# Matmul order in the four-tile passes of two expert mixtures around a slot-attention layer

## The chip, the core and the metric

The kernel runs on one core of a Trainium2 chip. A core has five engines with a program of their own each: TensorE (PE in the profile; PEld is its weight load), VectorE (DVE), ScalarE (ACT), GpSimd (POOL) and SyncE (SP, which here issues DMAs). Each takes its instructions in a fixed order and waits on semaphores for the others. The metric is the device time of one execution in microseconds, the median of the runs.

## The reference

Two sequences of 1024 tokens of 512 features go through three layers with residuals: half a mixture of two experts, an attention of 16 heads with 64 memory slots, and half a mixture again with the same weights. The mixture is what the change touches:

```python
h = jnp.einsum('nd,ehd->enh', x_flat, w_fc)                 # 512 -> 2048 hidden, two experts
a = jnp.square(jnp.where(h >= 0, h, 0.5 * h))
expert_out = jnp.einsum('enh,edh->end', a, w_proj)          # 2048 -> 512
mask = (top_idx[None, :] == jnp.arange(num_experts)[:, None]).astype(x.dtype)
out = jnp.einsum('end,en->nd', expert_out, mask * top_weight[None, :])
```

All is float32. A token uses one expert; the first `einsum` is called the first layer here and the second the second layer.

## The kernel before

**Passes.** Tokens are sorted by expert into a DRAM buffer. A mixture works through 17 tiles of 128 sorted tokens in six passes, each of which belongs to one expert. Lines 44 and 45 give the tiles of each pass: (2, 4, 2, 4, 1, 4) in the first mixture, (4, 4, 4, 2, 2, 1) in the last. Pass numbers count from 0. A pass runs over four chunks of 512 hidden features (`NHQ`, loop variable `ck`). For each chunk the weights `wfc` and `wp` are loaded by SP into a pool of 11 large buffers.

**Slow and fast passes.** Passes of one or two tiles use plain matmuls: `hidden` (bank hp, L514) and `project` (banks op, L735). Passes of four tiles use a scheme with seven block products in place of eight: `hidden_fast` (L598) for the first layer and `project_fast` (L664) for the second. Its operands are sums of blocks: T of tokens (DVE), S and R of the weights (POOL, L545 to L573), Q of the activations (DVE, `unit_sums`, L576). T, S, R share a pool of six buffers named sums, so POOL can make the sums of a later chunk only when an older sum has been used for the last time.

**One chunk of the first layer.** `hidden_fast` makes the four activations a of a chunk in two halves, q = 0 and 1. A half has seven products of two matmuls each, in banks named hU, hV and hC, and hands control back (`yield`) four times:

| step of a half | products on TensorE | what reads the banks |
|---|---|---|
| 1 | hU, hV, hC | ACT copies hU (kp or kv), DVE adds hC into hA (L627) |
| 2 | hU again, added to what is there | ACT copies hU (e) |
| 3 | hU again | ACT copies hU (uT), DVE adds it to hV into hB (L636) |
| 4 | hU again (hU<-T,wfc in the trace) | ACT copies hU into hB (L639), DVE t_b (L503), ACT a_b |
| 5 | hV again (hV<-xsT,S) | DVE adds hV and e into hA (L643), DVE t_a (L503), ACT a_a |

Steps 5 of q = 0 and 1 of q = 1 stand together, so a chunk has eight gaps where control comes back. The sums Q of a half are queued in `late` and issued behind the L627 add of the next half. hU and hV share two buffers of one pool, so the next half's hU and hV wait for the readers of the old ones. hU<-T, hV, hU, hV, hC, the last two products of a chunk and the first three of the next, are called a hand-over below.

**Between the steps.** The generator `pending` holds the second layer of the chunk before. `project_fast` has seven products of four matmuls, into banks that a reader empties (oa, in the two pools at and tr) and banks that gather over the pass (o), and yields after each matmul, 28 times. The loop at L794 takes three of these after each first-layer step of a fast pass; the rest follow after the last step (L814):

```python
for _ in steps:
    run(pending, 3 if fast else 0)
    run(ending, 1 if fast else 2)
    run(prep, 0 if early else 1 if fast else 2)
    yield ps, ck
```

`ending` is `finish_fast`, the last sums of the pass before (DVE), and `prep` transposes the tokens of the next pass in its last chunk (bank lt, in pool tr).

**What sets the order.** The program gives instructions with their data dependences. At build time a scheduler simulates the engines and gives each engine its final order: among the instructions that are ready in its simulation it takes the one that the source has first. So a later matmul can move ahead of an earlier one that waits. `tc.issue_after(x)` adds an edge without a wait: what is issued inside it stands behind x on x's engine. The attention layer chains all its TensorE instructions so (`on_pe`, L954); the mixtures do not. The last mixture's pass 0 runs interleaved with the end of the attention layer.

Of the kernel before, what the change touches and what calls it, by code (L numbers as in the profile page):

```python
# [15 lines left out]
P = 128  # L16
# [29 lines left out]
NPASS = 6  # L46
# [3 lines left out]
def tile_macaron(  # L50
# [14 lines left out]
    nc = tc.nc  # L65
# [15 lines left out]
    def large_tile(shape, name):  # L81
        return large.tile(shape, F32, tag="big", name=name)
# [139 lines left out]
    def small_t(shape, tag, name, dt=F32, bufs=2):  # L222
        return small.tile(shape, dt, tag=tag, name=name, bufs=bufs)
# [8 lines left out]
    class Mixture:  # L232
# [3 lines left out]
        def __init__(self, ph, plan, split):  # L236
            self.ph, self.rows, self.split = ph, None, split
            self.passes, self.groups = plan
            self.starts = [sum(self.passes[:j]) for j in range(NPASS)]
            self.e1 = small_t([P, NT], "e1", f"e1{ph}")  # L240
            self.run = small_t([P, NT], "run", f"run{ph}")
            self.before = small_t([P, NT], "bef", f"bef{ph}")
            self.pos = small_t([P, NT], "pos", f"pos{ph}", mybir.dt.int32)

            self.own = small_t([P, NPASS], "own", f"own{ph}")
            self.seen = self.ranked = self.done = 0
            self.deferred = not split

# [206 lines left out]
    def ffn(m, views):  # L457
# [36 lines left out]
        def activate(h, hc, nm, psum=False):  # L494
            n = h.shape[-1]
            t = work.tile([P, n], F32, tag="sq", name=f"t{nm}")
            if psum:

                r = work.tile([P, n], F32, tag="th", name=f"r{nm}")
                nc.scalar.activation(r, h, AF.Relu, scale=0.5)  # L500
                m.mark_dve = nc.vector.scalar_tensor_tensor(t, h, 0.5, r, ALU.mult, ALU.add)  # L501
            else:
                m.mark_dve = nc.vector.scalar_tensor_tensor(t, h, 0.5, h, ALU.mult, ALU.max)  # L503
            at = work.tile([P, n], F32, tag=A_TAGS[hc], name=f"a{nm}", bufs=3)
            nc.scalar.activation(at, t, AF.Square)
            return at
# [16 lines left out]

# [65 lines left out]
        def flush():  # L594
            while late:
                late.pop(0)()

        def hidden_fast(ps, ck, xT, T, wfc, S, a, sums):  # L598
            w = wfc.rearrange("p (k d h) -> p k d h", k=2, d=2)
            lo, hi = slice(0, 256), slice(256, 512)  # L600
            a += [None] * 4
            for q in range(2):
                nm = f"{ph}_{ps}_{ck}_{q}"
                first, second = ts(q, P), slice(256 + q * P, 256 + (q + 1) * P)
                U = ps2.tile([P, 256], F32, tag="pj", name=f"hU{nm}")
                V = ps2.tile([P, 256], F32, tag="pj", name=f"hV{nm}")
                C = ps1.tile([P, 256], F32, tag="st", name=f"hC{nm}")

                def product(bank, left, right, start):
                    for d in range(2):  # L610
                        m.mark = nc.tensor.matmul(  # L611
                            bank, lhsT=left[:, d, :], rhs=right[:, d, :],
                            start=start and d == 0, stop=d == 1, skip_group_check=True,
                        )

                def keep(name, bufs=2):
                    t = work.tile([P, 256], F32, tag=name, name=f"{name}{nm}", bufs=bufs)
                    nc.scalar.copy(t, U)  # L618
                    return t

                hA = work.tile([P, 512], F32, tag="oT", name=f"hA{nm}")
                hB = work.tile([P, 512], F32, tag="oT", name=f"hB{nm}")
                product(U, w[:, 0, :, first], xT[:, 0:2, lo], True)
                p1 = keep(("kp", "kv")[q], 1)
                product(V, S[0][:, :, first], T[0], True)
                product(C, w[:, 1, :, first], xT[:, 2:4, lo], True)
                added = nc.vector.tensor_tensor(hA[:, lo], C, p1, ALU.add)  # L627
                with tc.issue_after(added.ins):
                    flush()
                yield  # L630
                product(U, S[1][:, :, first], T[1], False)
                u2 = keep("e")
                yield
                product(U, S[2][:, :, first], T[2], False)
                u3 = keep("uT")
                nc.vector.tensor_tensor(hB[:, hi], V, u3, ALU.add)  # L636
                yield
                product(U, w[:, 1, :, second], T[3], False)
                nc.scalar.copy(hB[:, lo], U)  # L639
                a[q + 2] = activate(hB, q + 2, nm + "b")  # L640
                yield
                product(V, S[3][:, :, first], xT[:, 2:4, hi], False)
                nc.vector.tensor_tensor(hA[:, hi], V, u2, ALU.add)  # L643
                a[q] = activate(hA, q, nm + "a")
                late.append(lambda q=q: sums.append(unit_sums(ps, ck, q, a)))
# [18 lines left out]
        def project_fast(ps, ck, a, S, wp, R, p, raw):  # L664
            w = wp.rearrange("p (k q d) -> p k q d", k=2, q=2)
            lo, hi = slice(0, 256), slice(256, 512)
            nm = f"{ph}_{ps}_{ck}"
            if ck == 0:
                for i, (pool, tag) in enumerate(OP_TAGS[1:]):
                    p[i] = pool.tile([P, 2, 256], F32, tag=tag, name=f"o{i}_{nm}")  # L670
                p["sum"] = large_tile([P, 4, 2, 256], f"osum_{nm}")
            acc = p["sum"]


            def product(bank, left, right, first, last):
                for t in range(2):
                    for q in range(2):
                        nc.tensor.matmul(  # L678
                            bank[:, t, :], lhsT=left(q)[:, ts(t, P)], rhs=right(q),
                            start=first and q == 0 and (t == 0 or last),  # L680
                            stop=last and q == 1, skip_group_check=True,
                        )
                        yield

            def keep(i, left, right):
                yield from product(p[i], left, right, ck == 0, ck == NHQ - 1)

            def add(i, left, right):

                pool, tag = ((ps2, "at"), (ps1, "tr"))[i % 2]  # L690
                bank = pool.tile([P, 2, 256], F32, tag=tag, name=f"oa{i}_{nm}")
                yield from product(bank, left, right, True, True)
                if ck == 0:
                    nc.scalar.copy(acc[:, i], bank)
                else:
                    nc.vector.tensor_tensor(acc[:, i], bank, acc[:, i], ALU.add)

            yield from add(0, lambda q: a[q][:, lo], lambda q: w[:, 0, q, lo])
            yield from keep(0, lambda q: a[q + 2][:, lo], lambda q: w[:, 1, q, lo])
            yield from add(1, lambda q: S[q][1], lambda q: R[1][:, q, :])  # L700
            yield from keep(1, lambda q: S[q][3], lambda q: w[:, 1, q, hi])
            yield from add(2, lambda q: S[q][2], lambda q: R[2][:, q, :])
            yield from keep(2, lambda q: a[q + 2][:, hi], lambda q: R[3][:, q, :])
            yield from add(3, lambda q: S[q][0], lambda q: R[0][:, q, :])
# [42 lines left out]
        def run(steps, n):  # L747
            for _ in range(n if steps else 0):
                next(steps, None)

        pending = ending = None
        late = []
        for ps in range(NPASS):
            fast = PASSES[ps] == 4
            ops = {} if fast else []
            for ck in range(NHQ):
                if ps == 0 and ck == 0:
# [34 lines left out]


                for _ in steps:  # L794
                    run(pending, 3 if fast else 0)
                    run(ending, 1 if fast else 2)
                    run(prep, 0 if early else 1 if fast else 2)
                    yield ps, ck
# [23 lines left out]
                if fast:  # L822
                    pending = project_fast(ps, ck, a, products, wp, R, ops, raw)
                else:
                    pending = project(ps, ck, a, wp, ops, raw)
# [601 lines left out]
    for _ in norm:  # L1427
        pass
    last_steps = ffn(last_mixture, out_views)
    attention(att, last_mixture, last_steps, weight_steps)  # L1430
    for _ in last_steps:
# [46 lines left out]
```

## Time and profile before

| | |
|---|---|
| median of 3 runs | 2293.77 us (2293.19 to 2294.2) |
| profiled execution | 2291.76 us |
| span of that execution, first to last instruction | 2290.1 us |
| mean granted TensorE clock | 0.996 |
| HBM traffic over the span | 97 GB/s |
| first mixture, fast pass 1 | 84 to 181.5 us |
| first mixture, fast pass 3 | 250.3 to 343.6 us |
| first mixture, fast pass 5 | 382.2 to 488 us |
| attention layer | from about 488 us to about 1870 us |
| last mixture, fast passes 1 and 2 | 1934 to 2031 and 2031 to 2129 us |

Times in the trace count from the first instruction of the span. An answer of the timeline names, for each group, its start, its duration, the engine, the line, the operation, the tile written and the tiles read, the shapes and how many records it has; in brackets stands how long the engine had been idle and what ended it. A float32 matmul leaves two records. Records of TensorE overlap, since matmuls are pipelined: the distance from one start to the next is the time that a matmul costs, 0.43 us for two records of 256 columns. The number behind a tile's name is left out, so hU stands for the hU of every chunk.

### The profile page before, as it was taken

How to read it: one execution, taken by the hardware profiler on the slowest of the kernel's cores; microseconds unless marked ns; L12 is line 12 of the kernel's file. 1: busy time of each engine (PE TensorE's matmuls, PEld its weight loads, DVE VectorE, ACT ScalarE, POOL GpSimd, SP SyncE). 2: the span in 40 equal slices, each digit the busy share in tenths (PEclk: the TensorE clock that was granted, in tenths of full speed). 3: DMA queues.
4: the chain of work that ended last, by engine and by line, in shares of the span. 5: the costliest groups of instructions: out<-in, count | busy, mean ns of one | idle time of the engine just before them, and what ended most of it. 6: DMA issues, size and time to landing. Idle time of an engine off the chain costs nothing.

```text
span 2290.1 us, 28873 instructions
## 1 busy us (share of the span) xinstructions
PE 2224.7 (97%) x10776; PEld 1533.8 (67%) x10776; DVE 1360.2 (59%) x3124; ACT 778.4 (34%) x1526; POOL 473.2 (21%) x400
## 2 busy tenths in 40 slices
PE   6999999999999999999999999999999999999998
PEld 5687687866556656655665656656655678888765
DVE  6554555656556656666865655755657777675311
ACT  2222222323434343444443433443433332222222
POOL 3523615301101101100101000000001345444000
PEclk9999999999999999999999999999999999999999
DMA  7615525331221311310312110210110303322442
GB/s 285 232 59 205 195 77 223 115 124 37 90 90 56 134 47 65 106 70 24 129 56 74 56 41 29 74 33 19 56 38 1 111 33 148 126 86 102 170 175 102
DMA packets 56940, 222.75 MB, mean 97 GB/s; under 512 B 5983, under 2 KB 13151, under 8 KB 38880
## 3 DMA queue, kind: packets, MB, share of 16 engines
q1 hardware_dynamic: 51232, 203.52, 25.1%
q0 software_dynamic: 5280, 16.85, 1.9%
q8 instruction: 86, 1.41, 0.2%
q10 hardware_dynamic: 288, 0.52, 0.1%
q14 instruction: 54, 0.44, 0.1%
HBM read 189.86 MB, written 31.54 MB: 97 GB/s over the span
## 4 chain that ended last, share of the span: by engine, by line
PE 75%; DVE 13%; issue 6%; ACT 2%; POOL 2%; DMA 1%; SPq 1%; another core or an unknown queue 0%; POOLq 0%; DVEq 0%; ACTq 0%
PE U L956 9%; PE po L956 7%; PE oa L678 7%; PE hU L611 6%; PE kU L956 6%; PE o L678 5%; PE V L956 5%; PE pq L956 4%; PE hp L514 4%; PE hV L611 3%; PE op L735 3%; PE C L956 2%; PE svp L956 2%; PE AB L956 2%; PE ok L956 2%
## 5 line engine op out<-in xcount | busy, mean ns | idle before, releaser
L1253 POOL TENSOR_TENSOR sg<-sg,ms 128x512 f32<-128x512 f32 x64 | 68.5, 1071 | 1147.3 <-DVE ms L1251 1062.2
L956 PE MATMUL po<-wo,oT 128*128 128x512 f32 x512 | 230.3, 592 | 0.0
L514 PE MATMUL hp<-xsT,wfc 128*128 128x256 f32 (+1 forms) x768 | 150.7, 351 | 8.1 <-DVE t L501 3.6
L956 PEld LDWEIGHTS po<-wo,oT 128*128 128x128 f32 x512 | 94.8, 190 | 93.7 <-issue 91.8
L514 PEld LDWEIGHTS hp<-xsT,wfc 128*128 128x128 f32 x768 | 128.3, 193 | 32.0 <-issue 10.6
L735 PE MATMUL op<-wp,a 128*128 128x512 f32 x320 | 143.2, 593 | 0.0
L1249 ACT ACT_TABLE_LOAD x63 | 80.8, 1283 | 146.8 <-DVE ms L1248 140.8
L501 DVE SCALAR_TENSOR_TENSOR t<-hp,r 128x256 f32<-128x256 f32 (+1 forms) x96 | 36.3, 378 | 154.1 <-ACT r L500 151.9
L956 PE MATMUL U<-vgT,X 128*128 128x512 f32 x256 | 120.3, 592 | 0.0
L1149 DVE RECIPROCAL rC<-CT 128x256 f32<-128x256 f32 x64 | 112.2, 1753 | 2.2
L956 PE MATMUL pq<-xnT,wq 128*128 128x512 f32 x256 | 113.0, 592 | 0.0
L956 PE MATMUL kU<-ksT,X 128*128 128x256 f32 x384 | 102.1, 388 | 1.4 <-DVE E L1049 1.4
L735 PEld LDWEIGHTS op<-wp,a 128*128 128x128 f32 x320 | 59.7, 190 | 60.9 <-issue 57.2
L611 PE MATMUL hU<-xsT,wfc 128*128 128x256 f32 x384 | 99.2, 380 | 0.7 <-ACT e L618 0.7
L1179 DVE TENSOR_REDUCE mx<-ts 128x4 f32<-128x256 f32 x64 | 27.0, 422 | 106.1 <-PE ts L956 105.9
L956 PEld LDWEIGHTS pq<-xnT,wq 128*128 128x128 f32 x256 | 48.3, 190 | 59.3 <-issue 58.6
L956 PEld LDWEIGHTS kU<-ksT,X 128*128 128x128 f32 x384 | 67.9, 190 | 27.1 <-issue 12.5
L500 ACT ACTIVATE r<-hp 128x256 f32<-128x256 f32 (+1 forms) x96 | 33.2, 347 | 154.9 <-PE hp L514 151.0
L1182 ACT ACT_TABLE_LOAD x63 | 80.8, 1283 | 1.1
L611 PEld LDWEIGHTS hU<-xsT,wfc 128*128 128x128 f32 x384 | 71.7, 190 | 13.7 <-issue 3.5
L956 PEld LDWEIGHTS U<-vgT,X 128*128 128x128 f32 x256 | 48.6, 190 | 47.5 <-issue 45.9
L1100 ACT COPY kET<-tk 128x512 f32<-128x512 f32 x64 | 37.4, 585 | 125.7 <-PE tk L956 125.7
(301 smaller groups left out, 5075.7 us busy)
## 6 DMA issues: line engine op xcount, KB each, us to landing
wfc<-in_w_fc_dram SPq DMA_DIRECT2D x48, 1024.0 KB, 5.0
wp<-in_w_proj_dram SPq DMA_DIRECT2D x48, 1024.0 KB, 6.7
vgT<-vgs SPq DMA_DIRECT2D x16, 1024.0 KB, 5.2
wv<-in_w_v_dram SPq DMA_DIRECT2D x8, 1024.0 KB, 6.0
ksT<-kss SPq DMA_DIRECT2D x8, 1024.0 KB, 5.0
wo<-in_w_o_dram SPq DMA_DIRECT2D x8, 1024.0 KB, 4.8
xs<-xs SPq DMA_DIRECT2D x6, 1032.0 KB, 5.1
wks<-in_w_ks_dram SPq DMA_DIRECT2D x24, 256.0 KB, 3.1
```

The source lines that it names most:

```text
L500: nc.scalar.activation(r, h, AF.Relu, scale=0.5)
L501: m.mark_dve = nc.vector.scalar_tensor_tensor(t, h, 0.5, r, ALU.mult, ALU.add)
L514: m.mark = nc.tensor.matmul(hp, lhsT=wfc[:, dc * HQ + hc * P : dc * HQ + (hc + 1) * P], rhs=xT[:, dc, :], start=(dc == 0), stop=(dc == DC ...
L611: m.mark = nc.tensor.matmul(bank, lhsT=left[:, d, :], rhs=right[:, d, :], start=start and d == 0, stop=d == 1, skip_group_check=True,)
L678: nc.tensor.matmul(bank[:, t, :], lhsT=left(q)[:, ts(t, P)], rhs=right(q), start=first and q == 0 and (t == 0 or last), stop=last and q == ...
L735: nc.tensor.matmul(ops[j], lhsT=a[hc][:, ts(j, P)], rhs=wp[:, ts(hc, D)], start=(ck == 0 and hc == 0), stop=(ck == NHQ - 1 and hc == HQ // ...
L956: att.pe = op(*args, **kw)
L1100: nc.scalar.copy(u.kET, tp)
L1149: nc.vector.reciprocal(u.rC, u.CT)
L1182: nc.scalar.activation(u.u, u.u, AF.Exp)
L1249: nc.scalar.activation(ms, ms, AF.Sqrt, bias=eps, scale=1.0 / DV)
L1253: u.gated = then.gated = nc.gpsimd.tensor_tensor(sg, sg, ms.to_broadcast([P, HG, DV]), ALU.mult)
```

## The change

A helper `in_order` chains matmuls as `on_pe` does, for both layers of fast passes, while `m.alone` is true: in passes 0 to 4 of the first mixture and in passes 1 to 5 of the last. Fast among these are passes 1 and 3 of the first mixture and passes 1 and 2 of the last, four of the six fast passes. Transposes and the matmuls of slow passes are not chained. In all six fast passes the loop takes four matmuls of `pending` after each step instead of three, a whole product.

```diff
@@ class Mixture
             self.deferred = not split
+            self.pe, self.alone = None, False
@@ ffn
+        def in_order(op, *args, **kw):
+            with tc.issue_after(m.pe.ins) if m.pe else nullcontext():
+                r = op(*args, **kw)
+            m.pe = r if m.alone else None
+            return r
@@ hidden_fast
-                        m.mark = nc.tensor.matmul(
-                            bank, lhsT=left[:, d, :], rhs=right[:, d, :],
+                        m.mark = in_order(
+                            nc.tensor.matmul, bank, lhsT=left[:, d, :], rhs=right[:, d, :],
@@ project_fast
-                        nc.tensor.matmul(
-                            bank[:, t, :], lhsT=left(q)[:, ts(t, P)], rhs=right(q),
+                        in_order(
+                            nc.tensor.matmul, bank[:, t, :], lhsT=left(q)[:, ts(t, P)], rhs=right(q),
@@ the loop over passes
             fast = PASSES[ps] == 4
+            m.alone = ps < NPASS - 1 if m.split else ps > 0
@@ the loop over steps
-                    run(pending, 3 if fast else 0)
+                    run(pending, 4 if fast else 0)
```

## The prediction

> **What bounds the kernel now.** I read engine shares first, then the table by stretch, then TensorE's timeline at places where one chunk of the hidden layer hands over to the next.
>
> ```profile
> PE 2224.7 (97%) x10776; PEld 1533.8 (67%) x10776; DVE 1360.2 (59%) x3124; ACT 778.4 (34%) x1526; POOL 473.2 (21%) x400
> ...
> PE 75%; DVE 13%; issue 6%; ACT 2%; POOL 2%; DMA 1%; SPq 1%; another core or an unknown queue 0%; POOLq 0%; DVEq 0%; ACTq 0%
> ```
>
> TensorE is busy for 97% of the span and carries 75% of the chain that ended last. The four stretches the change orders (passes 1 and 3 of the first mixture, 1 and 2 of the last) have even less air:
>
> ```profile
> 84.00:181.50 97.50, 95.22 (x425) 78.71 (x424) 58.13 (x90) 25.57 (x57) 41.68 (x30) 1.00 0.29 104
> 250.30:343.60 93.30, 92.55 (x414) 77.40 (x413) 48.89 (x83) 24.09 (x54) 34.04 (x26) 1.00 0.28 98
> 1934.00:2031.00 97.00, 96.63 (x455) 84.46 (x454) 67.59 (x106) 25.27 (x56) 46.72 (x36) 1.00 0.28 95
> 2031.00:2129.00 98.00, 97.58 (x457) 85.58 (x456) 62.15 (x101) 25.18 (x55) 40.25 (x30) 1.00 0.29 102
> ```
>
> Length and TensorE's busy time come first, then PEld, DVE, ACT, POOL, the granted clock (1.00). Idle: 2.3 + 0.75 + 0.4 + 0.4 = 3.8 us of 386. The change removes no matmul, so it can win about that, and every new wait on this engine lengthens the run.
>
> **What covers a hand-over today.** One hand-over of pass 1 of the last mixture (columns: start, duration, engine, line, op, records, idle before):
>
> ```profile
> 2000.24 1.03 PE L611 MATMUL hU<-T,wfc 128*128 128x256 f32 x4
> ...
> 2001.36 0.37 ACT L639 COPY hB<-hU 128x256 f32<-128x256 f32 x1 [1.79 <-PE hU L611]
> ...
> 2001.76 0.69 DVE L503 SCALAR_TENSOR_TENSOR t_1b<-hB 128x512 f32<-128x512 f32 x1 [1.06 <-ACT hB L639]
> ...
> 2002.40 1.03 PE L611 MATMUL hV<-xsT,S 128*128 128x256 f32 x4
> ...
> 2003.46 0.42 DVE L643 TENSOR_TENSOR hA<-hV,e 128x256 f32<-128x256 f32 x1 [1.01 <-PE hV L611]
> ...
> 2004.99 1.03 PE L611 MATMUL hU<-xsT,wfc 128*128 128x256 f32 x4
> ...
> 2005.23 1.27 POOL L553 TENSOR_TENSOR S<-wfc 128x512 f32<-128x512 f32 x1 [14.79 <-PE oa L678]
> ...
> 2005.85 1.03 PE L611 MATMUL hV<-T,S 128*128 128x256 f32 x4
> ```
>
> A first-layer product is four records, 0.86 us from its start to the next. Three second-layer matmuls (1.30 us) lie between 2001.10 and 2002.40, four (1.73 us) between 2003.26 and 2004.99. The next chunk's hV at 2005.85 can start only when DVE has run t_1b and then the add hA that reads the old hV; hA ended at 2003.88, two microseconds early. Those seven matmuls are the cover.
>
> **The change, part by part.** A second-layer chunk is 7 products of 4 matmuls, 28; a first-layer chunk offers 8 gaps. Three per gap used 24 and left 4 for the end: every gap and the hand-over had filler. Four per gap use all 28 in seven gaps. The eighth, between the last hU<-T and the last hV, is empty, and so is the hand-over: hU<-T, hV, hU, hV, hC run bare. The order edges forbid pulling later matmuls into the hole. Other gaps grow from 1.30 to 1.73 us; they had no wait, so nothing is gained.
>
> *Hand-overs.* The bare sequence stands once in the trace, from 261.50 in the first mixture's pass 3: hV at 262.36, hU at 263.23, hV at 264.09, hC at 265.02. Three products took 2.66 us for 2.59: cost 0.07, with t_0b at 0.69. It stands again in pass 1, beside weight sums on POOL:
>
> ```profile
> 106.36 1.13 PE L611 MATMUL hV<-xsT,S 128*128 128x256 f32 x4 [0.22 <-DVE hB L636]
> ...
> 106.58 2.89 DVE L503 SCALAR_TENSOR_TENSOR t_1b<-hB 128x512 f32<-128x512 f32 x1 [0.27 <-ACT hB L639]
> ...
> 109.95 1.10 PE L611 MATMUL hV<-T,S 128*128 128x256 f32 x4 [1.60 <-DVE hA L643]
> ```
>
> There it cost 109.95 - 107.33 - 0.86 = 1.76. So ends of 0.07 and 1.76, and what decides is whether POOL runs beside t_1b. Between them is the commonest disturbed case:
>
> ```profile
> 2027.45 1.27 POOL L567 TENSOR_TENSOR R<-wp 128x512 f32<-128x512 f32 x1 [16.97 <-PE hU L611]
> ...
> 2027.86 1.40 DVE L503 SCALAR_TENSOR_TENSOR t_1b<-hB 128x512 f32<-128x512 f32 x1 [1.06 <-ACT hB L639]
> ```
>
> 1.40 for 0.69 adds 0.71: a disturbed hand-over costs 0.78. The Trainium skill ("SBUF — State Buffer", section on SBUF's two sides) speaks against this harder: a DVE instruction with two SBUF inputs and a GpSimd one exclude each other for a whole instruction. With POOL starting 1.3 us ahead (below), t_1b waits out the second POOL instruction (1.60, L554) and ends about 1.7 later than alone: 1.7 a hand-over. The row shows half of that; I take the row and keep 1.7 for the range.
>
> Which are disturbed? Two already have t_1b at 1.40 (1928.60, 2027.86). Five more have POOL waiting for a freed sums buffer, which comes just after t_1b today: on hV at 130.78, 293.31, 1979.33 and 2078.64, on oa at 2005.23. The last seven-product matmul (R's last use) now ends before hU<-T instead of after hV, so I expect an R buffer to free first and POOL to start about 1.3 us before t_1b. Seven at 0.78 and five at 0.07 make 5.8. Behind the waiting hV stand hC and the next chunk's products. a_1a, needed 3.0 us after hV ends, takes 0.62 + 0.04 + 0.69 + 0.04 + 0.63 + 0.05 = 2.1: hidden.
>
> *First chunk of passes 1 and 3, first mixture.* The filler there is the two-tile pass before: 8 matmuls of 512 columns. They fill two gaps instead of three, and today's schedule then pulls hC and the next chunk's second-layer matmuls forward; the edges forbid that. A bare step from hU to hU costs: ACT's copy starts 0.20 after the product's end (259.98 after 259.78), lasts 0.37, restart 0.07, 0.64 in all. Three such steps are 1.9. The last hV of the chunk waits for hB behind four sums Q (0.42 + 1.49 + 1.49 + 0.43 in that stretch): about 1.1. With 0.1 more in pass 3 that is 3.1, against 1.4 lost there today (0.57 + 0.07 + 0.73); in pass 1 the same list, 0.2 more at the first hV and its 1.6 hand-over (t_1b 2.89) make 4.9 against 3.2 (0.25 + 0.39 + 1.76 + 0.55 and some 0.3 of slips). Together +3.5; ends 0 (the sums slip) and +6.
>
> *Smaller.* In the last mixture's passes 1 and 2, finish_fast's DVE instructions (0.69 each, at 1953.11 and 1954.32) lie around t_1b at the first hand-over; with no cover one of them shows in part, 0.3 each, 0.6 (ends: -0.8, the 0.42 and 0.37 waits on hA at 2044.19 and 1944.88 vanish; +1.4). In four last chunks a transpose's copy (0.58) must clear bank tr one product before oa needs it: 0.1 each, 0.4. First-mixture pass 5 and last-mixture pass 0 get the new count without edges; the schedule can still fill holes: 0, ends -2 and +2. SP's weight loads: wp is released up to 2 us earlier, nobody waits. The slow passes' hp matmuls keep their order; their second bank is wanted 2.6 us after the last hV starts; hA is done at 1.5 (2003.88 after 2002.40).
>
> *Sum.* 5.8 + 3.5 + 0.6 + 0.4 = +10.3. The profiled execution took 2291.76 (span 2290.1 and 1.7 around it), so 2302.1; the median of the runs stands 2.0 above that execution: **2304**.
>
> **Rivals.** Measurement here can tell about 0.2%, 4.6 us, from nothing.
>
> *No visible change.* POOL's five starts do not move early and the sums slip out of the way: 2 hand-overs at 0.78, ten at 0.07, half of the first-chunk cost: 1.6 + 0.7 + 1.75 = 4.0, so 2298. For it: three of four ordered passes have no wait after their first chunks. Against: the empty gap is certain arithmetic. Chance 0.20.
>
> *Faster.* One mechanism: whole products free the oa banks and let their DVE adds run early, so DVE is clear when hB and hA come. Pass 5's first chunk now waits 2.85 + 0.40 + 0.21 (402.05 on hB, 405.75, 393.75), pass 0's 0.71 + 0.88 (1897.32, 1916.61). All of it gone, plus the 0.79 of hA waits, is -5.8, with hand-overs at 0.07 -5.0: 2289. It decides only if t_1b is never disturbed and the first chunks cost nothing. Against: the 2.85 comes from Q at 3.54 beside POOL, which no order of matmuls touches. Chance 0.10.
>
> *Clearly slower.* The lock as the skill states it: 7 at 1.7 and the rest as above, 11.9 + 0.35 + 4.5, so 2311; if a_1a also comes late, 2316. Chance 0.15.
>
> *The forecast*: 0.55. The order edges take effect in any case, because nothing else can hold the matmuls.
>
> **How the numbers follow.** Slower holds forecast and last rival, 0.70; same 0.20; faster 0.10. The range starts at 2293 (hand-overs at 0.07, first chunks 0, unordered passes -2) and ends at 2316.
>
> **What would show it.** Right: bare hU<-T, hV, hU, hV, hC at each hand-over, hV waiting for DVE hA L643 about ten times, S or R on POOL starting before t_1b, t_1b's median above 0.69; idle of TensorE up by some 1.7 in each of passes 1 and 3, 3 in the last mixture's two. Wrong: t_1b stays at 0.69 and hV waits under 0.1 (no visible change), or the waits of pass 5 are gone (faster).

## The result, and the profile after

| | before | after |
|---|---|---|
| median of the runs | 2293.85 us (8 runs) | 2301.37 us (8 runs) |
| lowest to highest | 2292.97 to 2296.16 | 2299.33 to 2305.42 |
| profiled execution, its span | 2291.76, 2290.1 | 2305.42, 2303.7 |
| mean granted clock | 0.996 | 0.994 |

The ratio is 1.0033, with a 95% interval of 1.0024 to 1.0041: **7.5 us slower**, where 10.3 were forecast. The profiled execution is the slowest of the eight, so sizes taken from it are on the large side. Lines of the kernel after are about ten higher (all chained matmuls of both layers carry L529, the helper's line).

First the shares and the chain of the page, then the table by stretch for the four ordered passes (length, then the busy time of TensorE, its weight load, VectorE, ACT and POOL, the granted clock, the DMA share and GB/s):

```profile
PE 2234.1 (97%) x10776; PEld 1536.2 (67%) x10776; DVE 1363.2 (59%) x3124; ACT 779.6 (34%) x1526; POOL 474.9 (21%) x400
...
PE 75%; DVE 13%; issue 6%; ACT 2%; POOL 2%; DMA 1%; SPq 0%; another core or an unknown queue 0%; POOLq 0%; DVEq 0%; ACTq 0%
```

```profile
86.10:193.30 107.20, 100.87 (x434) 82.01 (x433) 60.10 (x91) 25.86 (x57) 37.86 (x29) 0.97 0.27 91
261.68:358.60 96.92, 95.42 (x430) 79.25 (x429) 49.00 (x86) 24.49 (x55) 34.14 (x26) 1.00 0.28 97
1943.00:2043.40 100.40, 99.87 (x465) 85.94 (x465) 69.33 (x108) 26.60 (x57) 50.74 (x37) 1.00 0.30 100
2043.40:2145.00 101.60, 101.11 (x470) 87.56 (x469) 64.96 (x105) 26.84 (x58) 43.74 (x31) 1.00 0.32 104
```

The page's shares tell nothing of the change. The table does: idle of TensorE is 6.3, 1.5, 0.5 and 0.5 us where it was 2.3, 0.75, 0.4 and 0.4, and only in the first stretch has the clock fallen, to 0.97.

A finer measure is used from here on. From each distance between two starts on TensorE I take off what a record of that width costs undisturbed (216 ns for 256 columns, 430 for 512, 110 for 128); the rest is **loss**, be it a wait or half clock. Summed by place, in the profiled execution of each kernel (the labels are those of the experiments below):

| loss in us | before | after | e_edges | e_four | e_swap_r | e_first | v_best |
|---|---|---|---|---|---|---|---|
| pass 1, chunks 0 and 1 | 3.4 | 10.6 | 4.4 | 9.4 | 7.7 | 2.0 | 0.8 |
| pass 3, chunks 0 and 1 | 1.4 | 2.7 | 2.4 | 1.1 | 3.4 | 0.5 | 0.0 |
| pass 5, chunks 0 and 1 | 4.3 | 8.9 | 5.8 | 9.3 | 3.8 | 2.6 | 2.5 |
| later chunks of passes 1 and 3 | 0.1 | 0.9 | 0.1 | 0.9 | 0.9 | 0.9 | 0.1 |
| join of pass 5 with the attention (35 us) | 8.6 | 1.9 | 8.7 | 1.9 | 1.9 | 1.9 | 1.9 |
| last mixture, pass 0 | 10.9 | 10.3 | 10.9 | 10.4 | 11.0 | 10.4 | 12.6 |
| last mixture, passes 1 and 2 | 1.7 | 3.8 | 2.6 | 3.4 | 3.8 | 3.8 | 1.7 |
| slow passes 0 and 2 of the first | 20.0 | 23.7 | 19.7 | 20.0 | 18.5 | 16.6 | 17.7 |

Two rows between before and after were not on anybody's list: pass 5 lost 4.6 more, and its join with the attention layer 6.7 less. The last row is waits of hp for loaded weights and the half clock behind them; it varies by more than the change between kernels that have the same code there, and no argument below uses it.

**What became of the hand-overs.** A hand-over of pass 1 of the first mixture, on the timeline (start, duration, engine, line, operation, tiles, records, idle before):

```profile
139.82 1.03 PE L529 MATMUL hU<-T,wfc 128*128 128x256 f32 x4
...
140.07 1.27 POOL L563 TENSOR_TENSOR S<-wfc 128x512 f32<-128x512 f32 x1 [17.70 <-PE oa L529]
...
140.69 1.03 PE L529 MATMUL hV<-xsT,S 128*128 128x256 f32 x4
...
141.35 0.69 DVE L504 SCALAR_TENSOR_TENSOR t_1b<-hB 128x512 f32<-128x512 f32 x1 [2.17 <-ACT hB L649]
...
141.42 1.76 POOL L564 TENSOR_TENSOR S<-S,wfc 128x512 f32<-128x512 f32 x1
141.55 1.03 PE L529 MATMUL hU<-xsT,wfc 128*128 128x256 f32 x4
141.96 0.42 DVE L653 TENSOR_TENSOR hA<-hV,e 128x256 f32<-128x256 f32 x1
...
142.41 1.32 DVE L504 SCALAR_TENSOR_TENSOR t_1a<-hA 128x512 f32<-128x512 f32 x1
142.52 1.10 PE L529 MATMUL hV<-T,S 128*128 128x256 f32 x4
```

The bare sequence stands as forecast, and POOL starts S 1.28 us ahead of t_1b, as forecast too. But t_1b takes 0.69. POOL's first sum ended just before it, and the second, which follows 0.07 us behind t_1b, is the one that stretches, to 1.76. hV comes 0.97 after hU instead of 0.86, and with its second matmul the hand-over costs 0.18. Nearly all cost just that; t_1b is 0.69 in every ordered pass. What POOL stretches at about half of them is t_1a, to 1.31 or 1.32, and TensorE shows no wait for a_1a there.

**Where the time went.** The first chunk of pass 1, same view:

```profile
102.74 1.28 POOL L663 DMA_INDIRECT x<-xs  x1 [0.15 <-PE hU L529]
...
103.50 6.02 DVE L504 SCALAR_TENSOR_TENSOR t_0a<-hA 128x512 f32<-128x512 f32 x1
...
104.02 1.30 POOL L578 TENSOR_TENSOR R<-wp,R 128x512 f32<-128x512 f32 x1
...
105.25 1.29 POOL L580 TENSOR_TENSOR wp<-wp 128x512 f32<-128x512 f32 x1
...
106.47 1.28 POOL L581 TENSOR_TENSOR R<-wp,R 128x512 f32<-128x512 f32 x1
107.69 1.27 POOL L563 TENSOR_TENSOR S<-wfc 128x512 f32<-128x512 f32 x1
109.04 1.61 POOL L564 TENSOR_TENSOR S<-S,wfc 128x512 f32<-128x512 f32 x1
...
109.56 0.63 ACT L506 ACTIVATE a_0a<-t_0a 128x512 f32<-128x512 f32 x1 [5.50 <-DVE t_0a L504]
110.09 0.35 ACT L628 COPY e<-hU 128x256 f32<-128x256 f32 x1
...
110.50 1.17 PE L529 MATMUL hU<-xsT,wfc 128*128 128x256 f32 x4 [4.12 <-ACT e L628]
...
112.13 2.07 PE L529 MATMUL hU<-T,wfc 128*128 128x256 f32 x4 [0.46 <-ACT uT L628]
```

t_0a needs 0.69 and took 6.02. ACT's a_0a waits for it, ACT's copy e stands behind a_0a in ACT's queue although hU was ready, and TensorE waits 4.12 us for e. Its granted clock is then 0.50 from 111.5 to 118.3 us: 2.07 for a product of 1.03. Of the 10.6 us that chunks 0 and 1 of this pass lose, this wait is about 4 and the half clock about 3. In pass 5 t_0a took 6.13, with the same neighbours, and TensorE waited 4.5 us.

Read the distances on POOL. In this row each sum starts 0.06 or 0.07 us before the one ahead of it ends, with one exception: L564 needs what L563 makes, and starts 0.08 us after its end (107.69 + 1.27 = 108.96, then 109.04). The starts alone say the same: 1.23, 1.22 and 1.22 us from one sum to the next, then 1.35. In that gap t_0a gets in: it ends at 109.52, and L564 takes 1.61 in place of 1.27. **Theory A:** a VectorE instruction that has met such a row on POOL gets in only at a gap before a sum that depends on the one just ahead. **Theory B:** the holes that the order leaves on TensorE (hand-overs, bare steps) are the cost, and t_0a is chance.

### The profile page after: what moved, and what is told of

Same layout as the page of the kernel before. It is cut to its first block, busy times and chain, and to the rows that moved or that the text cites. A ratio compares the mean times of both kernels' runs of the same rounds, so it can differ in the third digit from the quotient of the medians.

```text
span 2303.7 us, 28852 instructions
## 1 busy us (share of the span) xinstructions
PE 2234.1 (97%) x10776; PEld 1536.2 (67%) x10776; DVE 1363.2 (59%) x3124; ACT 779.6 (34%) x1526; POOL 474.9 (21%) x400
## 4 chain that ended last, share of the span: by engine, by line
PE 75%; DVE 13%; issue 6%; ACT 2%; POOL 2%; DMA 1%; SPq 0%; another core or an unknown queue 0%; POOLq 0%; DVEq 0%; ACTq 0%
PE U L967 9%; PE po L967 7%; PE oa L529 7%; PE hU L529 6%; PE kU L967 6%; PE o L529 5%; PE V L967 5%; PE pq L967 4%; PE hp L515 3%; PE hV L529 3%; PE op L745 3%; PE C L967 2%; PE svp L967 2%; PE AB L967 2%; PE ok L967 2%
## 5 line engine op out<-in xcount | busy, mean ns | idle before, releaser
L529 PE MATMUL hU<-xsT,wfc 128*128 128x256 f32 x384 | 102.0, 388 | 4.6 <-ACT e L628 4.6
L529 PEld LDWEIGHTS hU<-xsT,wfc 128*128 128x128 f32 x384 | 73.8, 194 | 18.7 <-ACT e L628 5.4
L967 PEld LDWEIGHTS kU<-ksT,X 128*128 128x128 f32 x384 | 67.9, 190 | 25.3 <-issue 12.6
```

The costliest lines, as they stand in the source:

```text
L529: r = op(*args, **kw)
L967: att.pe = op(*args, **kw)
```

## The experiments

Every comparison ran the kernel before anew, with a median of 2293.86, 2293.31 or 2290.50 us; a gain or loss is taken within its comparison.

**Edges alone (e_edges), count alone (e_four).** Expected of the edges alone:

```diff
-                    run(pending, 4 if fast else 0)
+                    run(pending, 3 if fast else 0)
```

> The order edges alone, three matmuls a step as before. On every engine but TensorE the order is that of the kernel before, and TensorE's own differs only in the first chunks of passes 1 and 3 of the first mixture (no hC and second-layer matmuls ahead of their place) and in two single hC matmuls of the last mixture. If the prediction's view holds, that the edges forbid what fills the holes of these first chunks: about +2 us over before (half of its 3.5 us). If the cost of the change comes from whole products, four a step, or from VectorE waiting beside POOL: within 1 us of before, and no VectorE t_ over 3 us.

Measured: 2296.27 us against 2293.86 of before in the same comparison, ratio 1.0011 (1.0004 to 1.0017). +2.4, near the +2: pass 1 and pass 3 lost 1 us more each. The agreement is looser than it looks, because pass 5, which has no edges, also lost 1.5 us more in that trace. t_1b took 3.06 in pass 1, much as before (2.89).

Expected of the count alone, the helper with its edge taken out:

```diff
-            m.pe = r if m.alone else None
+            m.pe = None
```

> Four matmuls a step without the order edges. ACT, POOL and SP keep the order of the changed kernel, VectorE too but for two instructions. If the edges open the holes (prediction's view of the hand-overs), the schedule fills them here, hand-overs cost under 0.05 us and the time falls to within 2 us of before, 2296 or less. If the count opens them and nothing fills them: hand-overs at 0.18 us in all six fast passes, t_0a near 6 us in passes 1 and 5 again, and 2300 to 2302, as the whole change.

Measured: 2298.97, ratio 1.0025 (1.0016 to 1.0033), +5.1. The two parts add up: 2.4 + 5.1 = 7.5. The hand-overs cost 0.18 without edges too, and t_0a is again 6.02 and 6.13. So the count opens the holes, and the schedule, free to fill them, leaves them. Presumably nothing waits there in its own simulation; no run shows that.

**R's last two sums exchanged (e_swap_r).** Nothing else changes, on any engine:

```diff
-            G.tensor_tensor(b12, w[:, 1, :, hi], b12, ALU.subtract)
-            G.tensor_tensor(R[:, 2], w[:, 1, :, lo], R[:, 1], ALU.subtract)
+            with tc.issue_after(G.tensor_tensor(R[:, 2], w[:, 1, :, lo], R[:, 1], ALU.subtract).ins):
+                G.tensor_tensor(b12, w[:, 1, :, hi], b12, ALU.subtract)
```

> The changed kernel with the last two sums of each R on POOL exchanged; the order of every other engine is the same. In the trace of the changed kernel t_0a of the first chunk took 6.0 us in passes 1 and 5, beside an indirect DMA and four POOL sums that follow one another without a gap; it ended in the first gap, before a sum that needs the sum just ahead of it. If DVE gets in only at such a gap: here the gap comes after one sum (R's second; the third needs it), t_0a takes 0.5 + 1.3 + 0.7 = 2.5 us, TensorE's waits of 4.1 and 4.5 us in the two passes go to under 1, and the time falls by 4 us or more, to 2297 or less. If DVE merely loses by chance or by a rate: t_0a stays at 4 us or more, and the time at 2301.

Measured: 2294.25, ratio to before 1.0004 (0.9995 to 1.0012). The timeline of its pass 1:

```profile
100.19 2.38 DVE L504 SCALAR_TENSOR_TENSOR t_0a<-hA 128x512 f32<-128x512 f32 x1
...
100.71 1.30 POOL L578 TENSOR_TENSOR R<-wp,R 128x512 f32<-128x512 f32 x1
...
102.09 1.61 POOL L580 TENSOR_TENSOR R<-wp,R 128x512 f32<-128x512 f32 x1
...
103.58 1.13 PE L529 MATMUL hU<-xsT,wfc 128*128 128x256 f32 x4 [0.52 <-ACT e L628]
```

The gap has moved to 102.09, t_0a ends in it after 2.38 us (2.5 expected), and TensorE's loss at hU falls to 0.7. Two exchanged sums take back 7.1 of the 7.5 us. The wait under 1 us holds for the places named; another, of 2.5 us, stood at pass 1's last hV behind the sums Q, 1.5 us each beside POOL, so that pass keeps 7.7 us of loss.

**The hand-overs filled (e_spread):**

```diff
-                for _ in steps:
-                    run(pending, 4 if fast else 0)
+                for i, _ in enumerate(steps):
+                    run(pending, (4 if i < 4 or (ck == 0 and ps and PASSES[ps - 1] < 4) else 3) if fast else 0)
```

> The changed kernel with the 28 second-layer matmuls spread as 4, 4, 4, 4, 3, 3, 3, 3, so that no gap is empty; edges stay, and the first chunk behind a two-tile or one-tile pass is as in the change. If the 7.5 us are hand-overs: their 18 places at 0.18 us go, about 3 us less, 2298, and nothing else changes. If they are the first chunks with t_0a near 6 us: 2300 to 2302, as the whole change.

Measured: 2302.75, ratio 1.0045 (1.0032 to 1.0059): no gain, and a little above the 2300 to 2302. Passes 1 and 2 of the last mixture did lose 2.4 us instead of 3.8, so hand-overs are worth what they cost; but t_0a was 6.02 and 6.12, and at the join 3.3 us of its gain were gone. The bare steps of the first chunks stayed in this run. As far as hand-overs go, theory B is too small.

**Is it the gap? A miss first (e_long).** In each S the third sum goes ahead of the second:

```diff
-            G.tensor_tensor(S[:, 1], S[:, 0], w[:, 0, :, lo], ALU.subtract)
-            yield
-            G.tensor_tensor(a21, w[:, 0, :, lo], a21, ALU.subtract)
+            with tc.issue_after(G.tensor_tensor(a21, w[:, 0, :, lo], a21, ALU.subtract).ins):
+                G.tensor_tensor(S[:, 1], S[:, 0], w[:, 0, :, lo], ALU.subtract)
+            yield
```

> The changed kernel with the third sum of each S on POOL put ahead of the second, so that the sum that needs the one just ahead of it comes two sums later. If a VectorE instruction that has met POOL gets in only at such a gap: t_0a of the first chunk goes from 6.0 us to 6.0 + 2 x 1.28 = 8.6 us in passes 1 and 5, TensorE's waits there grow by as much, and the time rises by some 4 to 5 us to about 2306. If t_0a ended after four sums for another reason (a limit in time, a change of the tile that POOL reads): 6 us as before, and 2301.

Measured: 2300.26, ratio 1.0035 (1.0021 to 1.0049), t_0a 6.02 and 6.13. The expectation failed. POOL's queue in that run shows what the edit had not done:

```profile
103.51 1.28 POOL L581 TENSOR_TENSOR R<-wp,R 128x512 f32<-128x512 f32 x1
104.73 1.27 POOL L563 TENSOR_TENSOR S<-wfc 128x512 f32<-128x512 f32 x1
106.08 1.61 POOL L564 TENSOR_TENSOR wfc<-wfc 128x512 f32<-128x512 f32 x1
```

L564 now overwrites what L563 reads. That is a dependence on the instruction just ahead as well, and the gap of 0.08 us is where it was. The run does not tell the theories apart. The next one (e_inter) removes every such pair:

```diff
+                    m.mix = ck == 1 and m.split
+                    for i, part in enumerate((S, R) * 5 if m.mix else (S,) * 5 + (R,) * 5):
...
+                            next(part)
```

(The two generators hand over after each sum, and an edge on POOL holds the order.)

> The changed kernel with the eight POOL sums of the second chunk of passes 1, 3 and 5 in the order S, R, S, R and so on, so that no sum needs the one just ahead of it; the order of TensorE, VectorE and ACT is the same. In the run with S's sums exchanged t_0a still ended after four sums: there the second of them overwrites what the first one reads, so the gap of 0.08 us had stayed. Here no such pair stands between the indirect DMA and the second sum of the next chunk, about seven sums of 1.28 us. If VectorE gets in only at a gap: one VectorE instruction with two SBUF inputs (t_0b or t_0a) takes 8 to 10 us in each of passes 1 and 5, and the time rises to 2305 or more. If something else ends the wait after four sums: 6 us or less, and 2302 or less.

Measured: 2304.18 against 2290.50 of before in that comparison, 13.7 us more, ratio 1.006 (1.0046 to 1.0074). Pass 1:

```profile
95.21 1.01 POOL L664 DMA_INDIRECT x<-xs  x1 [0.77 <-DVE mw L470]
...
95.79 9.06 DVE L472 TENSOR_SCALAR mw<-mw 128x2 f32<-128x2 f32 x1
96.23 1.30 POOL L534 TENSOR_TENSOR S<-S,wfc 128x512 f32<-128x512 f32 x1
...
102.33 1.26 POOL L534 TENSOR_TENSOR R<-wp,R 128x512 f32<-128x512 f32 x1
103.56 1.25 POOL L534 TENSOR_TENSOR S<-wfc 128x512 f32<-128x512 f32 x1
...
104.89 1.26 POOL L534 TENSOR_TENSOR S<-S,wfc 128x512 f32<-128x512 f32 x1
...
107.08 1.22 PE L529 MATMUL hV<-T,S 128*128 128x256 f32 x2 [8.76 <-DVE hA L654]
```

Another victim than expected, a tiny instruction on two columns, but the same pattern: it waits 9.06 us through seven sums without a gap and ends 0.04 us before the dependent sum at 104.89. TensorE waits 8.76 us behind it. In pass 5 t_0b took 6.84, from where it met the row of sums to the next gap; eight were expected there. Theory A stands for these rows. Two rivals of e_long's expectation are gone: neither a limit of 6 us nor a change of the tile that POOL reads, which comes at every sum here, let VectorE in.

**Where theory A holds.** Not every row of independent sums holds VectorE. In the kernel after, a microsecond after t_0a was released:

```profile
110.61 1.44 POOL L566 TENSOR_TENSOR wfc<-wfc 128x512 f32<-128x512 f32 x1
110.86 1.48 DVE L600 TENSOR_TENSOR Q<-a_0a 128x256 f32<-128x256 f32 x1
...
112.02 1.48 POOL L567 TENSOR_TENSOR S<-wfc,S 128x512 f32<-128x512 f32 x1
```

L567 needs nothing of L566 and starts 0.03 us before its end, yet Q, 0.42 to 0.43 us long alone, gets in between: it ends at 112.34, and L567 takes 1.48. Over all 14 traces I counted the joints of two independent sums at which a t or Q of VectorE (or the mw above) stood waiting. Where an indirect DMA stood ahead in the same row, with no dependent sum since, VectorE got in at none of 33 joints (13 waits, all in the first chunks of passes 1 and 5 of the first mixture). Everywhere else it got in at all 693, so that it waited for the rest of one sum. The long wait thus goes with a row behind an indirect DMA. That the DMA causes it is not shown: no run moved the DMA alone.

**The first chunk's filler (e_first).** The changed kernel, edges and POOL as they are:

```diff
-                    run(pending, 4 if fast else 0)
+                    run(pending, (1 if ck == 0 and ps and PASSES[ps - 1] < 4 else 4) if fast else 0)
```

> The changed kernel, edges and POOL's order kept, with one matmul a step in the first chunk behind a one-tile or two-tile pass. If the loss needs the coincidence of t_0a with the DMA and the sums, which four matmuls a step bring about: t_0a falls under 3 us without any change on POOL, and the time to 2287 (2283.8 of the kernel with R exchanged and no edges, and up to 2.4 for the edges). If POOL's order is needed as well: 2293 or more.

Measured: 2282.14 against 2290.50, ratio 0.9962 (0.9948 to 0.9975): 8.4 us faster than before. Its TensorE in pass 1:

```profile
86.59 1.03 PE L529 MATMUL hU<-T,S 128*128 128x256 f32 x4
87.45 1.02 PE L745 MATMUL op<-wp,a 128*128 128x512 f32 x2
88.31 1.03 PE L529 MATMUL hU<-xsT,wfc 128*128 128x256 f32 x4
89.17 1.02 PE L745 MATMUL op<-wp,a 128*128 128x512 f32 x2
90.03 1.02 PE L529 MATMUL hU<-T,wfc 128*128 128x256 f32 x4
```

One filler of 0.86 us between any two hU covers the copy of 0.64. t_0a is 0.69 in all twelve chunks of this mixture: the products that the DMAs of the pass before wait for are spread too, POOL has a pause from 92.86 to 95.22, and t_0a (95.31) falls on the start of the DMA behind it and meets no row of sums. The 6-us wait thus needs both, t_0a falling on the row, as it does when the filler is spent in two gaps, and the gapless row on POOL; either remedy removes most of it. The 8.4 us against before are not all due to the filler, though: by the table 6.7 us of loss are gone at the join of pass 5, and the kernel after has gained these as well. What the filler did to the kernel after is 8.4 + 7.5, some 16 us.

**Towards the best version.** Three more kernels without edges and with R exchanged. The count four everywhere (v_four_swap, the edits of e_four and e_swap_r together):

> Four matmuls a step, no order edges, the last two sums of R exchanged. The three parts found so far add up: whole change 2301.4, minus 7.1 by the exchange, minus about 2.4 by the edges of the first chunks: 2292, 2 us faster than before. If the edges' cost was that of this exchange's place only (a coincidence of POOL and VectorE): 2294, as with the edges.

2290.70 against 2293.31, ratio 0.9990 (0.9982 to 0.9999). The parts add up within 1.3 us. Then one a step in the first chunks (v_first, with the edit of e_first):

> As four matmuls a step without edges and with R's sums exchanged, but one 512-column matmul a step, not four, in the first chunk behind a one-tile or two-tile pass, so that each of the eight gaps (four of them in pass 5) holds one. If the remaining cost of these chunks is bare hU to hU steps of 0.64 us: they vanish, 3 to 4 us less in passes 1, 3 and 5 together, about 2289. If it is VectorE beside POOL: the waits move to other places and the time stays at 2292 within 1.

2283.79 against 2293.31, ratio 0.9962 (0.9948 to 0.9976): more than expected, the chunks 0 and 1 of the three passes lost 5.6 us instead of 11.2. This is the cleanest measure of the spread filler: 6.9 us against v_four_swap in the same comparison. Then three as before, and four only in pass 5 (v_last):

```diff
-                    run(pending, 4 if fast else 0)
+                    run(pending, (4 if ps == NPASS - 1 else 3) if fast else 0)
```

> Three matmuls a step as before and no edges, four only in the last pass of the first mixture, and R's sums exchanged. In the trace of before the join of that pass with the attention layer loses 1.6 + 3.4 us to adds of VectorE queued behind the pass's last sums, and some more to the half clock that follows; in every trace with four a step the join loses 0.7. If the count in this one pass does it: about 6 us less there, the rest as before, 2287 to 2290. If the gain at the join comes from all four passes (what is late arrives earlier): 2292 or more.

2286.26 against 2293.31, ratio 0.9966 (0.9954 to 0.9978): a little under the 2287 to 2290, with a loss of 1.9 us at the join: the join's gain comes from this one pass. It is another queue on VectorE. In the kernel before:

```profile
497.21 0.68 DVE L716 TENSOR_TENSOR osum<-osum 128x512 f32<-128x512 f32 x1
...
498.01 0.69 DVE L718 TENSOR_TENSOR osum<-ou,osum 128x512 f32<-128x512 f32 x1
...
498.61 2.74 DVE L723 SCALAR_TENSOR_TENSOR xs<-osum,mw,xs 128x512 f32<-128x512 f32 x4
...
501.26 0.42 DVE L1049 TENSOR_TENSOR E<-kU,kv 128x256 f32<-128x256 f32 x1
...
501.74 1.65 PE L956 MATMUL kU<-ksT,xnT 128*128 128x256 f32 x3 [3.26 <-DVE E L1049]
```

The attention's add E, whose operand from TensorE was ready, stands behind the last sums and the output of pass 5, 4.1 us of work, and TensorE waits 3.26 us (the granted clock is 0.50 from 500.0 to 506.8). In the kernel after, four matmuls a step leave the end of pass 5 between other products, its last sums come later, and E goes ahead of them:

```profile
513.72 0.42 DVE L1060 TENSOR_TENSOR E<-kU,kv 128x256 f32<-128x256 f32 x1
514.06 0.68 DVE L721 TENSOR_TENSOR osum<-o,osum 128x512 f32<-128x512 f32 x1
...
514.97 1.03 PE L967 MATMUL kU<-ksT,xnT 128*128 128x256 f32 x4
```

Last, the union: one a step in the first chunks, four in pass 5, three elsewhere (v_best); and the same with the last two sums of S exchanged as R's are (v_best2).

```diff
-                    run(pending, 4 if fast else 0)
+                    run(pending, (1 if ck == 0 and ps and PASSES[ps - 1] < 4 else 4 if ps == NPASS - 1 else 3) if fast else 0)
```

> No edges, R's last two sums exchanged; one matmul a step in the first chunk behind a one-tile or two-tile pass, four in the last pass of the first mixture, three elsewhere. Against the kernel with four elsewhere (2283.8) the empty gap and the bare hand-overs of four passes go, 12 at 0.18 us, and 0.1 at the transposes: 2281. If three a step loses elsewhere what it wins (pass 0 of the last mixture lost 1 us more with three in the runs so far): 2283.

> As the run before it, and the last two sums of S exchanged as R's are, so that the gaps on POOL lie at most three sums apart. If VectorE's waits beside POOL still cost: another 1 us less, 2280. If the rest of them are covered by TensorE's work: no change, within 1 us.

2280.08 (ratio 0.9957, 0.9943 to 0.9971) and 2280.18 (0.9954, 0.9941 to 0.9968), both against 2290.50. **10.4 us faster than before**, the lowest ratio with v_best2, though its interval overlaps those of e_first and v_first; its loss in chunks 0 and 1 of passes 1 and 3 is 0.8 us in place of 4.8. Each against before in its own comparison, it won 0.9 us more than v_first (9.5), where 2.8 or 0.8 were expected; the intervals, some 3 us each way, do not tell the two cases apart. S's exchange adds nothing, as expected if the rest is covered.

## Why the prediction was right, and where it was not

Direction and size came out (10.3 forecast, 7.5 measured), but by other terms than the sum had. That the sum came near is luck: the largest term was too large by more than half, a lock of 6 us was missing in two passes, and a gain of 6.7 us that nobody forecast made up for most of it. One of the prediction's own signs of being wrong did come, t_1b at 0.69.

- *Hand-overs, 5.8 forecast.* Twelve at 0.18 are 2.2. The step that failed is "Seven at 0.78". POOL did start 1.3 us ahead, but this spared t_1b instead of disturbing it: S and R begin with two dependent sums, and t_1b met the gap between them. Even the two that the kernel before has at 1.40 fell to 0.69. A count of overlaps was not enough; the phase decides. The disturbance moved to t_1a, and a_1a still came in time, as the prediction's sum of 2.1 us had it.
- *First chunks of passes 1 and 3, 3.5 forecast (its two differences of 1.7 make 3.4).* Pass 3 lost 1.3 more in chunks 0 and 1, where 1.7 were forecast: the bare steps cost 0.62 each as read off. Pass 1 lost 7.2 more (5.4 to 6.1 in e_long, e_four and e_spread), where 1.7 were forecast. The bare steps were there; the lock on t_0a was not in the sum, though it stood in the trace of before under other names, t_1b at 2.89 and Q at 3.54, each behind an indirect DMA and a row of sums. I had moved these two along unchanged and not asked what sets their length.
- *Unordered passes, 0 forecast (−2 to +2).* Two large terms of opposite sign: pass 5's chunks +4.6, its join −6.7, pass 0 of the last mixture −0.6. The sum of −2.7 lies just outside the ends.
- *finish_fast 0.6, transposes 0.4.* The last mixture's two ordered passes lost 2.1 more in all, of which eight hand-overs are 1.4; the waits for hA at the first hand-over were 0.63 and 0.66, 0.1 more than before, so that finish_fast cost 0.2 and not 0.6. A transpose's bank costs 0.08.
- *"The order edges forbid pulling later matmuls into the hole."* True in the first chunks (2.4 us with the two hC of the last mixture). At the hand-overs the edges do nothing: the same order comes without them.
- *The lock as the Trainium skill states it* ("SBUF — State Buffer", the section on SBUF's two sides) was put aside for the row with 1.40. Its rule says that whichever starts first holds the shared ports for its whole instruction. The rule was not harsher than the row; the prediction applied it at the wrong phase. The row agrees with it: t_1b started 0.41 us behind R (2027.45) and ended 0.54 after R's end. So does the hand-over at 139.82: t_1b (141.35) starts first and takes 0.69, and the sum behind it (141.42) is the one that waits. The 1.7 each had t_1b meet the second sum in progress. At the first chunk the rule is too mild: t_0a waited out four sums, not one, in a row behind an indirect DMA.
- *Why a row can act as one.* "GPSIMD Engine Reference" of the same skill (2.1, Instruction dispatch) says that a POOL instruction may start while parts of the one before still run, unless it waits for it. In the rows that held VectorE independent sums overlap by 0.04 to 0.08 us and dependent ones stand 0.08 apart, which agrees. That the ports stay taken across the overlap is my inference, and the overlap alone is not enough: elsewhere sums overlap by about 0.04 us too, and VectorE got in.

Of the rivals, "faster" named the waits of pass 5's first chunk going away. The loss in its chunks 0 and 1 grew from 4.3 to 8.9 us; what went away was the wait at its join, which it had not named.

## What to carry to other kernels

Before a bare stretch is called cheap, look for what VectorE has there beside POOL, and at which phase. In these traces the wait was the rest of one POOL instruction, except in a row behind an indirect DMA: there it was all POOL instructions up to the next one that depends on its neighbour. Spread a small amount of filler one piece to a gap rather than whole products to a few; covering a step of 0.64 us takes 0.86 us of work, and a second piece in the same gap covers nothing. A change that only reorders must be followed to the joins with the next stage, where the order of another engine's queue can turn over.

## What the runs showed that I had not expected

- One VectorE instruction stretched from 0.69 to 6.02 us, and one on 128x2 elements to 9.06, by a row of independent sums on POOL of 1.28 us each behind an indirect DMA; adds that read a bank of TensorE were not held (hA took 0.42 at 141.96 beside a sum in the kernel after, hB 0.42 at 95.45 in e_inter beside the indirect DMA).
- Both waits began while an indirect DMA ran on POOL, about 0.5 us before the first sum of the row. Others of the kind began after its end: t_1b of before at 106.58 (2.89 us; the DMA ended at 106.39) and t_0b of e_inter in pass 5 (6.84 us, begun 2.4 us behind the DMA's end). In e_first t_0a ran its 0.69 us within the first 0.78 us of such a DMA. So the wait goes with the row behind the DMA, not with the DMA's own time; what sets such a row apart stays open.
- After the wait of 4.1 us in pass 1 TensorE ran on at a granted clock of 1.00 for 0.9 us, and then had 0.50 for 6.8 us. In pass 5 the clock was 0.50 from 411.8, 2.2 us before TensorE came back from its wait of 4.5 us, again for 6.8 us.
